# A recurrent layer and a mixture of experts on one core: more PSUM banks for the tiles, six weight places, a new written order

## The chip, the core and the metric
The kernel runs on one core of a Trainium2 chip. The core has five engines that run their own instruction streams and wait for each other by semaphores: TensorE (PE; its weight loads are shown apart as PEld), VectorE (DVE), ScalarE (ACT), GpSimd (POOL) and SyncE (SP). Here SP only issues DMAs, POOL issues the indirect DMAs (scatters), and DMA engines move the data. TensorE writes into PSUM, of which this kernel uses eight banks of 128 partitions x 512 floats; the other engines copy results from there into SBUF. The metric is the time of one execution on the device, in microseconds (us).

## The reference
All is in float32, x is 4 x 512 tokens of 256 features. First x + attention(layernorm(x)), then x + ffn(layernorm(x)):

```python
# attention: a gated linear recurrence with complex state
xh = x @ W_in + b_in
gate_x = sigmoid(block_diag_linear(xh, W_gx, b_gx))      # 8 blocks
gate_a = sigmoid(block_diag_linear(xh, W_ga, b_ga))
a = exp(complex(-8 * gate_a * softplus(a_real), a_imag * gate_a))
xc = sqrt(1 - a * a) * complex(xr, xi) * gate_x          # xr, xi: the halves of xh
h = linear_scan(a, xc)                                    # over the 512 tokens
out = concat(h.real, h.imag) @ W_out + b_out
# ffn: 32 experts in 8 groups; each token takes its best 6 out of its best 4 groups
scores = sigmoid(xf @ gate_w.T)
w, idx = top 6 of the scores in the best 4 groups; w = w / sum(w) * 2.5
y = sum over the token's experts e of w[e] * (silu(x @ w11[e].T) * (x @ w33[e].T)) @ w22[e].T
shared = (silu(xf @ sw1.T) * (xf @ sw3.T)) @ sw2.T
return y + shared
```

An expert's inner size is 128, the shared expert's is 2 x 128.

## The kernel before
**Stage 1, per batch b of 512 tokens.** `tokens_of`, `gates`, `angles`, `turned` and `scans` (named g, a, f and s with the number of the batch) compute the recurrence: statistics of the tokens (L335), the input product (L393), the gates, the angles' sine and cosine on ACT and DVE (L405 to L475), the scans on DVE. `attend` and `scored` (t) add the residual with transposes by the identity (L603) and the output product, normalize (L349), transpose (pt, L357) and compute the router's scores (pl, L516). `route` (r) picks the experts on DVE, computes a position `pos` for each of a token's six copies and lets POOL scatter the token's row of 320 floats (256 features, its weights, its place) into the table `xg` in DRAM, where each expert has an area of its own (L578). That is 24 scatters of 128 rows for a batch, 96 in all. In batches 0 and 1 a small memset on POOL (L588, 0.41 us) follows each scatter, to keep them at a distance. `shared` (h) computes the shared expert (sg and su at L637, sy at L646) and stores it to DRAM through SP (512 KB, L648).

**Tables.** `tables` (L650 to L717) turns the counts of tokens by expert into tables of tiles: which expert a tile of 128 rows belongs to, and where its rows lie. It is made twice: "ne" after batch 2 for the first 40 tiles (EARLY), "nl" for the others after batch 3. Each time it is a chain of some 20 small DVE operations with three PE operations between them: the count pc, a transpose ptt (L703) and a broadcast pb (L710).

**Stage 2, the tiles.** 112 tiles in 56 pairs p. Names: l, x, k, u, d.
- `read` (l, L820): SP loads a pair's rows from `xg`, two DMAs of 160 KB; four pairs ahead (AHEAD). Pairs 0 to 19 wait for the 72 scatters of batches 0 to 2, later ones for all 96.
- `spread` (x): four transposes on PE into one bank `pxt` (L836), a copy by ACT (L838) into one of two SBUF buffers, and four DVE operations, oh, pick, cd and place (L841 to L848).
- `weights` (k, L856): two DVE copies of an expert's w11 and w33 out of `w_all`, chosen by a register, into the next of the places `b_w`. Place number is tile number modulo the count of places, which is four here.
- `up` (u): eight matmuls into `gu` (L868), of two PE instructions each in the profile (16 rows), silu on ACT (L870), a multiply on DVE (L872).
- `down` (d): two matmuls into one bank `y` (L881; four rows in the profile), two ACT copies with the routing weight as scale (L885) into one of six places `b_y` (u, p, th, kk, s, c in turn), and two scatters by POOL into `zz` (L887).

Beside some pairs, `own_read` (o) loads the residual and the shared expert's result of a batch (2 x 512 KB) and `own_sum` (q, L923, 1.22 us on DVE) adds them.

**Last stage.** Once all scatters into `zz` have landed, `zz` is loaded in 16 DMAs into `w_all` (17 us on the chain), DVE sums the six results of a token (L978, L980), PE transposes them together with the own sum (pz, L984, L985), ACT copies (L987), SP stores.

**PSUM.** The eight banks belong to pools: ps_a has two ("a": stage 1's transposes and products, the tables' ptt and pb, the last stage's pz), ps_x two ("x1": the residual of stage 1, the last shared expert's sy), ps_s two ("gu"), ps_m one ("m": pxt) and ps_y one ("y").

**The order.** Nothing is left to a scheduler's taste: `ORDERS` is a written list for each engine, such as "x0:4 x1:4 u0:8", which reads: four instructions of x0, four of x1, eight of u0. `in_order` ties each instruction to the one before it on its engine. So an instruction that waits holds up all that stand behind it in its engine's list.

Of the kernel before, what the change touches and what calls it, by code (L numbers as in the profile page):

```python
# [9 lines left out]
F32 = mybir.dt.float32  # L10
# [9 lines left out]
P = 128  # L20
B, T, D = 4, 512, 256
KC = D // P
# [34 lines left out]

ORDERS = {
    ET.PE:
        "g0:8 t0:7 g0 t0 g0:15 g1:23 g2 g1 g2:5 t0:5 g2:2 t0:15 t1:2 t0 t1 t0 t1 t0:2 t1:4 t0:8 h0:3 g2:2 h0 g2 r0:2 g2 "  # L60
        "r0:4 g2:12 h0:2 g3:8 h0 t1:2 h0 t1:14 h0:8 t1:8 h1:2 t1 t2:2 t1 h1 t1:6 r1:2 t2:5 h1 g3:2 t2 g3:6 r1:4 g3:5 h1 "
        "g3:3 t2:3 h1 t2:13 h1:9 t2 h1 t2:8 h2:4 t2:7 r2 h2:4 r2:5 t3:3 h2:2 t3 ne h2 t3:2 h2:5 t3:9 ne t3:3 d0 t3:2 ne "
        "t3:13 h3 t3 h3:3 t3:6 h3 r3 h3:3 r3:5 h3:8 x0:4 x1:4 u0:8 u1:2 x2:4 u1:6 x3 u2 d0 x3 d0 x3 u2 x3 u2:5 d1 u2 d1 "
        "nl x4:2 u3:4 x4:2 u3:2 d2 u3:2 x5:4 u4 d2 u4:4 x6:3 u4:3 x6 d3:2 u5:3 x7:3 u5:3 x7 u5:2 u6:2 d4:3 u6:4 x8:4 "
        "u6:2 u7 d5:2 u7:3 x9:2 u7:2 x9:2 d6 u7:2 d6 u8:8 d7:2 u9:2 x10:4 u9:5 d8 u9 d8 x11:4 nl d8 u10:5 x12:4 u10 "
        "d9:2 u10:2 u11:8 x13:2 d10:2 u12 x13:2 u12:6 x14 u12 x14:3 u13:2 d11 nl u13:3 d11 x15:3 d12 x15 u13:3 u14:2 "
        "d12:2 u14 x16:4 u14:5 u15 d13 u15:2 d13 u15:5 x17:4 d14:2 u16:4 x18:2 u16 x18:2 u16:3 u17 d15 u17 d15 u17:6 "
        "d16 u18:6 x19:4 u18 d16:2 u18 u19:3 x20 u19 x20:3 u19 d17:2 u19:2 x21:2 u19 u20:2 x21:2 d18:2 u20:2 x22:4 "
        "u20:4 u21:2 d19:2 u21:6 u22 d20 u22:2 d20:2 x23 u22 x23:2 u22 x23 u22:3 d21:2 x24:2 u23 x24:2 u23:6 x25:2 u23 "
        "u24 x25:2 d22:2 u24:4 x26:4 u24 d23 u24 d23 u24 u25:8 d24:3 u26:6 x27:4 d25:2 u26:2 u27:3 x28:4 u27:2 d26:2 "  # L70
        "u27:2 x29:2 u27 x29:2 u28:6 x30:2 u28:2 x30 d27:2 x30 u29:6 d28 u29:2 u30 x31:2 d28 x31:2 d28 u30:7 d29:2 "
        "x32:4 u31:5 d30:2 u31:3 x33:4 u32:8 d31:2 d32 u33 x34:4 u33:7 u34:2 x35:4 d32:2 u34:6 x36:4 d33:2 u35:3 x37 "
        "u35:2 x37 u35:3 x37:2 d34:2 u36:8 d35:2 u37 x38:4 u37:7 u38 x39 d36:2 x39:2 u38 x39 u38 d36 u38:5 x40:4 u39 "
        "d37:2 u39:2 x41 u39:5 x41:3 u40:6 x42 d38:2 u40:2 x42:2 u41:4 x42 d39 u41:2 d39 x43 u41:2 d40 x43:2 u42:2 x43 "
        "u42:2 d40:2 u42 x44:2 u42 x44:2 u42:2 u43:4 d41 x45 d41 x45:2 u43:2 x45 u43:2 u44:3 d42:2 x46:2 u44 x46 u44:2 "
        "x46 u44:2 u45:2 d43:2 d44 u45 x47 u45:5 x47:3 d44 u46 d44 u46:7 x48:4 d45:2 u47:4 x49:2 u47:3 x49 d46 x49 d46 "
        "u47 u48:8 x50:3 u49:2 x50 d47:2 u49:2 x51 u49 x51 d48 x51 u49:2 x51 u49 d48:2 u50:7 d49:2 u50 u51 x52 u51 "
        "x52:3 u51:6 d50 x53:4 u52 d50 u52:7 d51 x54:4 d51 d52 u53:8 x55:2 d52:2 x55:2 u54:7 d53 u54 d53 u55:8 d54:2 "
        "d55:2",
    ET.DVE:  # L80
        "c cc:7 c:4 cc:2 c cc:5 g0 cc g0:6 c:2 cc:2 g0:2 c g0:13 c cc c g1 a0 g1 cc a0:2 g1 a0:2 cc g1:2 a0:3 g1:2 f0 "
        "g1 a0 g1 a0 g1 c g1:5 a0 g1:7 a0:2 f0 a0:3 f0 a0 f0:2 s0 a0:3 s0:8 g2 a1 g2:2 a1:2 g2:2 a1 t0 g2:2 t0 a1 t0 "
        "a1:3 f1 g2 t0:2 a1:2 t0:17 a1 f1 a1 f1 a1:4 f1 a1 f1 s1 r0:27 a1 r0:8 a1:2 s1:6 h0 f2 s1:2 g3 a2:2 g3:4 a2:5 "
        "t1 a2 t1 g3:2 h0 g3 a2 t1:13 r0 t1:7 a2 f2:2 a2:7 f2:2 s2 a2:2 r1:4 a2 r1:19 s2 r1:4 s2 r1:8 s2:4 r1 s2:2 a3:8 "
        "t2 h1 a3:2 t2 a3 t2:11 h1 t2:9 f3 a3 f3 a3:5 f3:3 s3 h2 a3:3 r2 s3:2 r2:5 s3 r2:30 h2 s3:2 ne s3:3 ne:16 k0 x0 "
        "t3:22 h3 k0 ne r3:25 h3 r3:9 x0 k0 k1 x0:2 k1 k2:2 u0 x1:4 r3:2 k3:2 x2:3 u1 k4 x2 x3:2 u2 k4:2 k5 x3:2 k5 "
        "x4:4 u3 k6 x5 u4 k6 x5:3 x6 k7:2 x6 k8 u5 k8 x6:2 x7 nl:2 u6 k8 k9 x7:3 x8:2 nl:2 k9 x8 nl x8 x9 nl u7 x9:3 "
        "x10 u8 x10 nl:2 k10 nl:10 k10 k11 x10:2 x11:4 u9 nl:2 k11 k12:3 u10 x12 nl k13:2 x12 q0 u11 x12:2 k14:2 x13:3 "
        "u12 u13 x13 x14 nl:2 k15:2 k16 x14 u14 nl x14 k16 x14 k16 x15:3 u15 k17:2 x15 x16:4 x17:2 u16 k18:2 k19 x17 "
        "k19 x17 u17 x18:2 k20 x18:2 k20 q1 x19:2 u18 x19 k20 u19 x19 x20 k21:2 k22:2 x20:2 u20 x20 x21:3 k23 x21 x22:2 "  # L90
        "u21 x22:2 x23:4 x24 k23 k24 q2 x24:2 k24:2 u22 x24 x25 u23 k25:2 k26:2 u24 k27 x25:3 x26:2 k27 u25 x26:2 k28 "
        "u26 x27:4 k28:2 k29:2 x28:3 u27 k30 u28 k30 k31:2 x28 x29:4 x30:2 u29 k32 u30 x30:2 x31:4 x32 k32:2 u31 k33:2 "
        "x32:3 x33 k34 x33:3 x34:2 u32 k34 k35:2 k36 u33 k36:2 x34:2 x35:3 u34 x35 x36 k37 x36:3 k37 u35 k38:2 x37:2 "
        "u36 x37:2 x38:4 x39 k39 u37 q3 x39:2 k39 k40:3 u38 x39 k41 x40:3 k41 x40 x41:2 u39 k42:2 u40 k43 x41 k43 x41 "
        "x42:2 k44 x42:2 x43 u41 x43:3 k44 x44:4 k44 k45 x45 u42 u43 u44 k45 k46:2 k47 x45:2 k47 x45 x46:3 u45 k48 x46 "
        "x47 k48:2 x47:2 u46 x47 x48:3 k49:2 u47 u48 k50 x48 x49:2 k50 u49 k51:2 x49:2 k52 x50:4 k52 x51:4 x52 u50 k52 "
        "u51 x52:2 k53:2 k54 u52 x52 x53 k54 x53:3 x54:4 x55:4 u53 k55:2 u54 u55",
    ET.Activation:
        "cc b0:2 g0:9 a0:2 g0:3 a0:8 g1:4 a0:2 g1:2 a0:2 g1:3 b1:2 g1 a1:2 b2:2 g1:2 a1:8 t0:4 p0:2 a1:2 t0:2 a1 t0 "
        "g2:4 a1 g2:4 h0 g2:2 a2:2 h0 b3:2 g2:2 a2:7 h0:2 t1:4 a2 t1 a2 t1 a2 p1:2 a2:2 t1 g3:7 h1 g3:2 a3:2 g3:3 a3 h1 "  # L100
        "a3:8 t2:4 h1 t2:2 a3 h1 a3 h2 a3 t2 p2:2 h2:3 t3:2 p3 t3:2 p3 t3:2 h3 t3 h3:2 x0 x1 u0 h3 x2 u1 d0:2 x3 u2 "
        "d1:2 x4 x5 u3 d2:2 x6 u4 d3:2 x7 u5 d4:2 u6 x8 d5:2 u7 x9 d6:2 u8 d7:2 x10 x11 u9 d8:2 d9:2 u10 x12 x13 u11 "
        "d10:2 x14 u12 d11:2 u13 x15 d12:2 x16 u14 d13:2 u15 x17 d14:2 u16 x18 d15:2 u17 x19 d16:2 u18 x20 d17:2 u19 "
        "x21 d18:2 x22 u20 d19:2 u21 d20:2 x23 u22 x24 d21:2 x25 u23 d22:2 u24 d23:2 x26 u25 d24:2 x27 d25 u26 d25 x28 "
        "u27 x29 d26:2 u28 x30 d27:2 u29 x31 d28:2 u30 d29:2 x32 u31 d30:2 x33 u32 x34 d31:2 x35 u33 d32:2 u34 x36 "
        "d33:2 u35 x37 d34:2 u36 d35:2 x38 u37 x39 d36:2 u38 x40 d37:2 x41 u39 d38:2 x42 u40 d39:2 x43 u41 d40:2 x44 "
        "u42 d41:2 u43 x45 d42:2 u44 x46 d43:2 u45 x47 d44:2 u46 x48 d45:2 x49 u47 d46:2 x50 u48 d47:2 u49 x51 d48:2 "
        "d49:2 u50 x52 u51 d50:2 x53 u52 x54 d51:2 u53 d52:2 x55 u54 d53:2 u55 d54:2 d55:2",
    ET.Pool:
        "c:10 r0:72 r1:71 r2:48 r3:24 d0:4 d1:4 d2:4 d3:4 r3:4 d4:4 d5:4 d6:4 d7:4 d8:2 r3:2 d8:2 r3:18 d9:4 d10:4 "  # L110
        "d11:4 d12:4 d13:4 d14:4 d15:4 d16:4 d17:4 d18:4 d19:4 d20:4 d21:4 d22:4 d23:4 d24:4 r1 d25:4 d26:4 d27:4 d28:4 "
        "d29:4 d30:4 d31:4 d32:4 d33:4 d34:4 d35:4 d36:4 d37:4 d38:4 d39:4 d40:4 d41:4 d42:4 d43:4 d44:4 d45:4 d46:4 "
        "d47:4 d48:4 d49:4 d50:4 d51:4 d52:4 d53:4 d54:4 d55:4",
    ET.SP:
        "c i0 c:3 i1 c:7 w:9 i2 w c:3 w c w:35 p0 w:19 i3 h0 p1 h1 p2 h2 l0 wl:7 p3 wl l0:2 l1:2 l2:2 l3:2 l4:3 l5:2 "
        "l6:2 l7:2 h3 l8:3 l9:2 l10:2 l11:2 o0 l12:3 o0 l13:2 o1 l14:2 l15:2 l16:3 l17:2 o1 l18:2 l19:2 l20:3 l21:2 "
        "l22:2 l23:2 o2:2 l24:3 l25:2 l26:2 l27:2 l28:3 l29:2 l30:2 l31:2 l32 o3 l32:2 l33:2 l34:2 l35:2 l36:3 l37:2 "
        "l38:2 l39:2 l40:3 o3 l41:2 l42:2 l43:2 l44:3 l45:2 l46:2 l47:2 l48:3 l49:2 l50:2 l51:2 l52:3 l53:2 l54:2 l55:2",
}


# [1 line left out]
def kernel(ctx, tc, x, w_in, w_gx, w_ga, vecs, w_out, gate, w11, w33, w22, sw1, sw3, sw2, out):  # L123
# [615 lines left out]
    for b in range(B):  # L739
        xh, gx, ga, u, p = made  # L740
# [34 lines left out]
    def again(tag, bufs, name, *shape):  # L775

        t = tmp.tile([P, *shape], F32, tag=tag, name=name, bufs=bufs)
        return t if len(shape) == 1 else t.rearrange("p a b -> p (a b)")
# [8 lines left out]
    b_gx, b_ga = again("gx", 2, "b_gx", T), again("ga", 2, "b_ga", T)  # L787
    b_sphi, b_cphi = again("sphi", 2, "b_sphi", T), again("cphi", 2, "b_cphi", T)
    b_y = [again(tag, 1, "b_" + tag, T) for tag in ("u", "p", "th", "kk", "s", "c")]
    b_w = [again(tag, bufs, "b_w" + tag, T) for tag, bufs in (("ph", 1), ("gx", 2), ("ga", 2), ("sphi", 2))]  # L790
    b_xt = [part_of(b_sphi, 0, 2, KC, P), part_of(b_cphi, 0, 2, KC, P)]
    b_silu = [part_of(b_gx, i, 2, P) for i in range(2)]
    b_act = [part_of(b_ga, i, 2, P) for i in range(2)]
# [33 lines left out]

    def spread(p):

        work(f"x{p}")  # L830
        rows = st[p][0]
        (_, et, had, _), t0 = of(2 * p)
        pt = ps_m.tile([P, 2, KC, P], F32, tag="m", name=f"pxt_{p}")
        for i in range(2):
            for k in range(KC):
                PE.transpose(pt[:, i, k], rows[:, i, k * P : (k + 1) * P], ident)  # L836
        xt = b_xt[p % 2]
        A.copy(xt, pt)  # L838
        oh = small.tile([P, 2, E], F32, tag="oh", name=f"oh_{p}", bufs=2)
# [35 lines left out]
    def down(p):  # L875
        work(f"d{p}")
        a, cd, place = st.pop(p)
        py = ps_y.tile([P, 2, D], F32, tag="y", name=f"y_{p}")
        for i in range(2):
            e = number(2 * p + i, 0, ET.PE, E - 1)  # L880
            m = PE.matmul(py[:, i], a[:, i], w2[:, bass.ds(e, 1)].rearrange("p o d -> p (o d)"), start=True, stop=True)  # L881
# [158 lines left out]
```

## Time and profile before

| what | value |
|---|---|
| median of 14 runs | 433.18 us (430.81 to 437.02) |
| the profiled execution | 433.95 us, span 432.0 us |
| busy in the span: PE, DVE, ACT, POOL | 350.1, 304.5, 234.6, 240.0 us |
| first scatter into `xg` issued | 80.71 us |
| last scatter of batch 2 issued, landed | 196.15, 198.64 us |
| first transpose of a tile, first matmul of a tile | 201.18, 204.95 us |
| last scatters into `zz` issued | 383.47 us |
| load of `zz` on the chain | 391.19 to 408.33 us |

The span goes from the first instruction to the last. The chain of work that ended last is followed back from the last instruction, at each step to what released it. In a table of waits, "A <- B" says that instructions A sat ready at the head of their engine until B ended. In a table of windows, the numbers behind each engine are the microseconds it was busy in that stretch and its instructions; the clock is TensorE's granted clock as a share of full speed. Of the 24 scatters of batch 3, twelve stand on POOL ahead of the first down result and the others among those of pairs 3 to 9.

### The profile page before, as it was taken

The numbers are of one execution on the slowest core, as the hardware profiler recorded it, in microseconds if no ns is written. First come the engines' busy times: TensorE is split into PE (matmuls) and PEld (weight loads), VectorE is DVE, ScalarE is ACT, GpSimd is POOL, SyncE is SP. The second block draws the span as 40 slices with busy tenths as digits, with TensorE's granted clock in tenths as the row PEclk, the third lists the DMA queues.
The fourth block names the chain that finished last, engine by engine and source line by source line (L and its number), as shares of the span: only waits on it lengthen the run. The fifth ranks groups of instructions, "written<-read, shape, count | busy, mean of one in ns | idle before, by whom it ended". The sixth has DMA issues, their size and how long they took to land.

```text
span 432.0 us, 7580 instructions
## 1 busy us (share of the span) xinstructions
PE 350.1 (81%) x2074; PEld 285.0 (66%) x2074; DVE 304.5 (70%) x991; ACT 234.6 (54%) x436; POOL 240.0 (56%) x269
## 2 busy tenths in 40 slices
PE   3925849997898878497999999999999999911394
PEld 3502336475636547355999999999999999911393
DVE  5179999999989997435668767766676576503883
ACT  2499699689769941341455455555555655510031
POOL 1000000498998998776777777777776667640000
PEclk9975988997999989779899999999999999975587
DMA  5799906524422344985877977946675564218995
GB/s 149 268 315 319 255 2 183 177 93 154 142 77 106 137 144 156 354 342 184 269 248 251 318 257 239 331 151 226 203 221 177 166 202 150 94 58 320 421 409 211
DMA packets 63580, 91.58 MB, mean 212 GB/s; under 512 B 8485, under 2 KB 53037, under 8 KB 63536
## 3 DMA queue, kind: packets, MB, share of 16 engines
q1 hardware_dynamic: 52400, 56.45, 41.3%
q0 software_dynamic: 9984, 28.33, 17.5%
q10 hardware_dynamic: 1152, 6.29, 3.6%
q8 instruction: 18, 0.29, 0.3%
q14 instruction: 26, 0.21, 0.2%
HBM read 51.19 MB, written 41.94 MB: 216 GB/s over the span
## 4 chain that ended last, share of the span: by engine, by line
PE 53%; DVE 20%; DMA 10%; ACT 8%; issue 5%; POOL 2%; ACTq 0%; SPq 0%; POOLq 0%; DVEq 0%
PE gu L868 22%; PE y L881 10%; PE pxt L836 5%; DMA w_all<-zz 4%; PE ph L393 3%; PE sg L637 2%; DMA zz<-b_u,place 2%; PE pz L984 2%; DMA xg<-row,pos 2%; PE pz L985 2%; POOL xg L578 1%; DVE st L335 1%; PE pt L357 1%; DMA x<-in_x_dram 1%; POOL zz L887 1%
## 5 line engine op out<-in xcount | busy, mean ns | idle before, releaser
L578 POOL DMA_INDIRECT xg<-row,pos x96 | 106.5, 1110 | 102.4 <-DVE w_all L474 78.3
L881 PE MATMUL y<-w_all,b_ga 128*128 x224 | 60.7, 381 | 0.9 <-ACT b_u L885 0.9
L872 DVE TENSOR_TENSOR b_ga<-b_gx,gu 128x256 f32<-128x256 f32 x56 | 23.4, 418 | 33.6 <-ACT b_gx L870 33.3
L881 PEld LDWEIGHTS y<-w_all,b_ga 128*128 128x128 f32 x224 | 36.9, 191 | 3.7 <-ACT b_u L885 1.3
L984 PE MATMUL pz<-ident,w_all 128*128 128x128 f32 x64 | 15.4, 330 | 27.9 <-DVE w_all L980 17.3
L870 ACT ACTIVATE b_gx<-gu 128x256 f32<-128x256 f32 x56 | 21.6, 385 | 29.0 <-PE gu L868 28.0
L868 PE MATMUL gu<-b_sphi,b_wgx 128*128 128x128 f32 x224 | 33.7, 281 | 0.0
L868 PE MATMUL gu<-b_cphi,b_wga 128*128 128x128 f32 x224 | 33.5, 278 | 0.0
L868 PE MATMUL gu<-b_sphi,b_wph 128*128 128x128 f32 x224 | 32.7, 277 | 0.0
L868 PE MATMUL gu<-b_cphi,b_wsphi 128*128 128x128 f32 x224 | 32.0, 275 | 0.0
L868 PEld LDWEIGHTS gu<-b_cphi,b_wga 128*128 128x128 f32 x224 | 30.9, 194 | 1.0
L984 PEld LDWEIGHTS pz<-ident,w_all 128*128 128x128 f32 x64 | 12.2, 237 | 28.9 <-DVE w_all L980 17.7
L868 PEld LDWEIGHTS gu<-b_sphi,b_wph 128*128 128x128 f32 x224 | 30.2, 192 | 1.1
L868 PEld LDWEIGHTS gu<-b_sphi,b_wgx 128*128 128x128 f32 x224 | 30.6, 197 | 0.5
L978 DVE TENSOR_TENSOR w_all<-w_all 128x768 f32<-128x768 f32 x16 | 15.1, 958 | 21.5 <-DMA w_all<-zz 21.4
L868 PEld LDWEIGHTS gu<-b_cphi,b_wsphi 128*128 128x128 f32 x224 | 29.1, 192 | 0.4
L987 ACT COPY o<-pz 128x256 f32<-128x256 f32 x16 | 5.9, 372 | 41.3 <-DMA w_all<-zz 26.9
L838 ACT COPY b_cphi<-pxt 128x512 f32<-128x512 f32 x28 | 16.4, 585 | 19.5 <-PE pxt L836 15.5
L838 ACT COPY b_sphi<-pxt 128x512 f32<-128x512 f32 x28 | 16.4, 586 | 15.4 <-PE pxt L836 13.0
L887 POOL DMA_INDIRECT zz<-b_u,place x20 | 20.0, 998 | 6.5 <-issue 2.1
L887 POOL DMA_INDIRECT zz<-b_p,place x20 | 20.0, 999 | 6.3 <-issue 1.7
L887 POOL DMA_INDIRECT zz<-b_th,place x18 | 18.3, 1018 | 8.6 <-ACT b_th L885 4.7
(331 smaller groups left out, 947.4 us busy)
## 6 DMA issues: line engine op xcount, KB each, us to landing
w_all<-in_w_dram SPq DMA_DIRECT2D x64, 128.0 KB
w_all<-zz SPq DMA_DIRECT2D x8, 768.0 KB
w_all<-zz ACTq DMA_DIRECT2D x8, 768.0 KB
xg<-blank SPq DMA_DIRECT2D x1, 5120.0 KB
b_xh<-xg SPq DMA_DIRECT2D x28, 160.0 KB
b_x<-xg SPq DMA_DIRECT2D x28, 160.0 KB
b_xn<-xg SPq DMA_DIRECT2D x28, 160.0 KB
b_xnt<-xg SPq DMA_DIRECT2D x28, 160.0 KB
```

The source lines that it names most:

```text
L393: PE.matmul(ph, win_sb[:, k, m * P : (m + 1) * P], xn[:, k], start=(k == 0), stop=(k == KC - 1))
L578: i = GP.indirect_dma_start(out=xg[:, :], out_offset=bass.IndirectOffsetOnAxis(ap=pos[:, t, k : k + 1], axis=0), in_=row[:, t], in_offset= ...
L637: PE.matmul(dst, w[:, i, k], xn2[:, k], start=(k == 0), stop=(k == KC - 1))
L836: PE.transpose(pt[:, i, k], rows[:, i, k * P : (k + 1) * P], ident)
L838: A.copy(xt, pt)
L868: PE.matmul(gu[:, w, i], w1[:, k, w], xt[:, i, k], start=(k == 0), stop=(k == KC - 1))
L870: A.activation(s, gu[:, 0], AF.Silu)
L872: V.tensor_tensor(a, s, gu[:, 1], ALU.mult)
L881: m = PE.matmul(py[:, i], a[:, i], w2[:, bass.ds(e, 1)].rearrange("p o d -> p (o d)"), start=True, stop=True)
L887: s = GP.indirect_dma_start(out=zz.rearrange("t k d -> (t k) d"), out_offset=bass.IndirectOffsetOnAxis(ap=place[:, i : i + 1], axis=0), in ...
L978: V.tensor_tensor(z[:, :half], z[:, :half], z[:, half:], ALU.add)
L984: PE.matmul(pt[:, k], z[:, 0, cut], ident, start=True, stop=False)
```

## The change
Three edits, and a new text of `ORDERS`.

```diff
-    b_w = [again(tag, bufs, "b_w" + tag, T) for tag, bufs in (("ph", 1), ("gx", 2), ("ga", 2), ("sphi", 2))]
+    b_w = [again(tag, bufs, "b_w" + tag, T) for tag, bufs in (("ph", 1), ("gx", 2), ("ga", 2), ("sphi", 2), ("cphi", 2))]
+    b_w.append(again("x", 2, "b_wx", KC, T)[:, :T])
...
     def spread(p):
...
-        pt = ps_m.tile([P, 2, KC, P], F32, tag="m", name=f"pxt_{p}")
+        more = p > 5 and p % 2
+        pt = (ps_a if more else ps_m).tile([P, 2, KC, P], F32, tag="a" if more else "m", name=f"pxt_{p}")
...
     def down(p):
...
-        py = ps_y.tile([P, 2, D], F32, tag="y", name=f"y_{p}")
+        more = p % 2
+        py = (ps_x if more else ps_y).tile([P, 2, D], F32, tag="x1" if more else "y", name=f"y_{p}")
```

So the transposes of odd pairs above 5 go to a bank of ps_a, the down results of odd pairs to a bank of ps_x, and the weight copies have six places, of which the two new ones lie in buffers of stage 1 that are free by then (42 of the 112 copies go there). The instructions are the same in number and kind; each engine's order is another. The parts around the start of the tiles, PE, DVE, POOL and SP in turn:

```diff
-h3:8 x0:4 x1:4 u0:8 u1:2 x2:4 u1:6 x3 u2 d0 x3 d0 x3 u2 x3 u2:5 d1 u2 d1 nl x4:2 u3:4 x4:2 u3:2 d2 u3:2 x5:4 u4 d2 u4:4
-x6:3 u4:3 x6 d3:2 u5:3 x7:3 u5:3 x7 u5:2 u6:2 d4:3 u6:4 x8:4 u6:2 u7 d5:2 u7:3 x9:2 u7:2 x9:2 d6 u7:2 d6 u8:8 d7:2
+h3:6 x0:4 h3:2 x1:4 u0:8 nl x2:4 u1:8 d0 x3:4 d0 u2:8 x4:4 d1 u3:6 d1 x5:4 u3:2 u4:2 d2:2 u4:6 d3 x6:2 d3 x6:2 d4 u5:8
+d4 nl u6:8 d4 nl x7:4 d5 x8:4 d5 d6:2 u7:5 x9 u7:3 x9:3 u8:2
...
-x4:4 u3 k6 x5 u4 k6 x5:3 x6 k7:2 x6 k8 u5 k8 x6:2 x7 nl:2 u6 k8 k9 x7:3 x8:2 nl:2 k9 x8 nl x8 x9 nl u7 x9:3
-x10 u8 x10 nl:2 k10 nl:10 k10 k11 x10:2 x11:4 u9 nl:2 k11 k12:3 u10 x12 nl k13:2 x12 q0 u11
+r3:6 x0 k0:2 k1:2 x0 r3:2 nl u0 k2 x0 x1:2 k2 k3 x1:2 k3 x2:2 u1 k4 x2:2 k4:2 x3:3 nl u2 x3 x4:2 nl:4 k5 nl k5 k6 x4 nl
+x4 u3 x5:2 k6 x5:2 x6 k7 nl x6 nl:6 u4 nl:3 k7 q0 k8 x6 nl:3 u5 x6 x7 k8:2 k9 u6 x7 nl:2 x7:2 x8:2 nl x8:2 k9 x9:2 k10:2 u7
...
-r2:48 r3:24 d0:4 d1:4 d2:4 d3:4 r3:4 d4:4 d5:4 d6:4 d7:4 d8:2 r3:2 d8:2 r3:18 d9:4 ... d24:4 r1 d25:4
+r2:48 r1 r3:22 d0:4 d1:4 d2:4 d3:4 d4:2 r3:6 d4:2 d5:4 d6:4 r3:16 d7:4 r3:4 d8:4 d9:4 ... d24:4 d25:4
...
-l4:3 l5:2 l6:2 l7:2 h3 l8:3 l9:2 l10:2 l11:2 o0 l12:3 o0 l13:2 o1 ... l32 o3 l32:2 ... l40:3 o3
+h3 l4:3 l5:2 l6:2 o0:2 l7:2 l8:3 o1 l9:2 l10:2 l11:2 l12:3 l13:2 o1 l14 o2 l14 l15 o2 l15 l16:3 ... l19 o3 l19 o3
```

(POOL and SP count two instructions to a scatter or a read.) In stage 1 the lists differ as well. On PE, two identity transposes of t0 instead of fourteen stand before the first pt of `gates`. On DVE, two memsets (L231, L238) stand before the first statistics. On ACT, batch 1's activation of L453 stands behind the normalization of batch 0's rows (L349) instead of ahead of it, and with it the later L459 and L465 of the same chain; the copies of batch 0's features (L358) still come behind L465. On SP one of the eight loads of w22 (wl) comes a little earlier.

## Prediction

> **What bounds the kernel now.** I began with the page's clock row and the summary of its chain of work that ended last:
>
> ```profile
> PEclk9975988997999989779899999999999999975587
> PE 53%; DVE 20%; DMA 10%; ACT 8%; issue 5%; POOL 2%; ACTq 0%; SPq 0%; POOLq 0%; DVEq 0%
> ```
>
> TensorE holds over half of the chain, with the clock full through most of the second half. An average over unlike stages says little, so I then asked for the windows (columns: length, PE, PEld, DVE, ACT, POOL busy, granted clock, DMA share, GB/s):
>
> ```profile
> 80.00:100.00 20.00, 19.79 (x76) 12.42 (x75) 19.40 (x44) 17.05 (x22) 17.59 (x22) 1.00 0.29 106
> 140.00:160.00 20.00, 15.38 (x58) 8.83 (x56) 19.08 (x56) 15.11 (x22) 18.14 (x23) 0.91 0.40 141
> 220.00:240.00 20.00, 20.00 (x156) 19.22 (x155) 15.27 (x68) 10.50 (x26) 15.26 (x16) 1.00 0.77 253
> 340.00:360.00 20.00, 20.00 (x158) 19.22 (x157) 11.22 (x38) 11.10 (x26) 12.93 (x14) 1.00 0.52 171
> ```
>
> From 220 to 360 us PE is busy 20.00 us in every 20 at a clock of 1.00: the tile stage is TensorE's own time. A pair of tiles is 16 gu rows (1.78 us), 4 y rows (0.87) and 4 transposes (0.44), 3.09 us; 56 pairs make 173 us, which is the distance from 204.95 us to the last matmul at about 378.8. A bank or a buffer more can take out of this only what PE waits for. So the third view is PE's waits from 180 to 405 us (total, times, longest):
>
> ```profile
> PE pz L984 <- DVE w_all L980: 17.3, 1, 17.3
> PE pt L357 <- ACT xs L624: 5.9, 1, 5.9
> PE pxt L836 <- DMA b_xh<-xg: 1.2, 2, 1.0
> PE pxt L836 <- DMA b_x<-xg: 1.1, 1, 1.1
> PE y L881 <- ACT b_u L885: 0.9, 1, 0.9
> PE pxt L836 <- ACT b_sphi L838: 0.8, 1, 0.8
> ```
>
> Two rows are waits for a PSUM bank, the last two, 1.7 us of 432. The others are for rows of tokens, the last stage's sum, and the router's input. Nothing here waits for a weight copy.
>
> What sets the start of the tiles is read from the chain in 172 to 240 us (start, length, what):
>
> ```profile
> 194.87 0.97 POOL xg L578
> 196.15 2.49 DMA xg<-row,pos
> 200.44 4.04 DMA b_x<-xg
> 204.51 0.44 PE pxt L836 x2
> 204.95 3.63 PE gu L868 x20
> ```
>
> The first tiles' reads wait for the 72 scatters of batches 0 to 2, which POOL issues one behind the other from 80.71 to 196.15. So three things can move the end: when POOL starts its scatters and how fast it goes, the ramp of the first tiles, and a new wait in a PE stream that has none.
>
> **Banks (pxt and py of odd pairs).** The 0.8 us is x1 waiting for the copy of x0 out of the one bank. After the change x1 still uses the old bank, as the new one is only for odd pairs above 5: gain 0. The 0.9 us is d55, which waits for ACT to empty d54's bank; d55 goes to a new bank, and the wait goes. But what is late next is POOL. The chain at the end shows:
>
> ```profile
> 378.25 0.97 POOL zz L887
> 380.91 8.47 DMA zz<-b_u,place
> ```
>
> POOL issues the last six scatters at 376.98, 378.25, 379.62, 380.91, 382.19 and 383.47, 1.28 us apart, and d55's two stand last whether their data is ready 0.9 us earlier or not. Gain 0 (at most 0.9, if POOL had caught up). In the middle there is no such wait to remove: 0. The last stage, from the scatters' landing to 432.0, keeps its instructions: 0.
>
> One rule of the Trainium skill speaks beside this: "TensorE: Matmul & The Clock Gate", section "HAM oscillation — how this bites in real kernels", reports that a second set of PSUM banks gave a stream already kept warm no further gain; by it too the banks are worth nothing, and this case's 20.00 of 20 says so with more right.
>
> **Six places for copied weights.** The 112 copies (L856, 128x512, 0.42 us) stay; 42 of them write the new places. PE's list has no wait for them, so 0. What hides a copy is PE's 3.09 us for a pair against DVE's work for it: two copies, the multiply (0.42) and the four small ones of spread (0.22, 0.29, 0.29, 0.16), 2.2 us.
>
> **Order of PE, tile start.** Two matmuls of the last shared expert (sy, 0.38 us each) move from before the first transposes to behind the first four. The short windows there, same columns:
>
> ```profile
> 203.00:204.50 1.50, 0.39 (x2) 0.15 (x2) 0.78 (x4) 0.00 (x0) 1.20 (x2) 1.00 0.89 242
> 206.00:207.00 1.00, 1.00 (x7) 1.00 (x6) 0.68 (x1) 0.00 (x0) 0.69 (x2) 0.50 1.00 371
> 209.00:210.00 1.00, 1.00 (x12) 1.00 (x11) 0.90 (x5) 0.59 (x1) 0.69 (x2) 1.00 0.43 159
> ```
>
> The clock is 0.50 from about 205.5 to 209.0, just behind a stretch, 201.0 to 204.5, in which PE was busy 1.29 of 3.5 us. Half rate for 3.5 us costs 1.75 us. The two matmuls raise 1.29 to 2.05. If that keeps the clock up, 1.75 us are won; if not, nothing; I take −0.4, nearer to nothing, since 2.05 of 3.5 is still a gap. The same page, section "Part 1: The HAM clock gate", would have the clock fall only after an idle window of about 3.4 us. No PE gap here was above 1.13 us, and it fell: the trace differs. By the page's rule the clock could not have fallen before and nothing could be won.
>
> **Order of DVE, PE and ACT in stage 1.** Batch 0's path to its positions: two memsets (L238 0.33, L231 0.17) stand before the first statistics, +0.50; twelve of the fourteen identity transposes that PE did ahead of the first pt go behind it (0.11 each at full clock, partly in PE's idle), up to −0.5; ACT's L453 of batch 1 (0.61, on the chain at 63.73) goes behind the normalization of batch 0's rows (L349), and so L465, behind which the copies of batch 0's features (L358) stand, waits longer for its input, 0 to +0.6; the rest of that path keeps its operations. So batch 0's positions come at −0.5 to +1.2; I take +0.8, nearer to the two costs that lie on the chain for certain. POOL goes without a break after that, so all of it reaches the tiles' start. Batch 1's positions are ready 0.1 us before POOL asks and have one 0.67 us operation less ahead of them, batch 2's have 4 us in hand: 0.
>
> How fast POOL goes is the unknown. Its groups, first from 80 to 167 us (batches 0 and 1), then from 167 to 200 (batch 2):
>
> ```profile
> L578 POOL DMA_INDIRECT xg<-row,pos x49 | 60.0, 1225 | 86.5 <-DVE w_all L474 78.3 <-issue 7.6 <-ACT so L647 0.5
> ...
> L578 POOL DMA_INDIRECT xg<-row,pos x25 | 24.6, 985 | 9.1 <-issue 8.2 <-ACT so L647 0.3 <-DMA xg<-row,pos 0.3
> ```
>
> The same instruction takes 1225 ns where DVE is busy 19 of 20 us and 985 where it is not: 48 × 0.24 = 11.5 us are lost beside DVE. The new order puts other DVE operations beside other scatters. Which, no row tells; the sum of DVE's work is the same, so I take 0, and a third of the loss, 3.8 us, to either side.
>
> "SBUF — State Buffer", section "Who interferes with whom", of the skill gives the cause: GpSimd and some DVE operations lock each other out of a shared port. It names 620 ns against some 3100. By that ratio a scatter beside DVE would be five times as long; the 1225 beside 985 says a quarter, so the row decides.
>
> **Order of DVE, tile start.** The tables for later tiles (22 or so operations, starts 0.14 apart in before at 233.38 to 235.65) and the first sum of shared results (L923, 1.22 us) move from beside pairs 7 to 15 to beside pairs 0 to 7, ahead of multiplies that PE's d4, d5 and d6 wait for. Between u3's last matmul and u4's PE needs u4 1.78 + d2 0.43 = 2.2 us. DVE in that time has x5's four (1.02), two copies (0.84), two of x6 (0.57), seven of the table (about 1.1) and u4's multiply (0.42), 3.9; it falls back 1.7. From u4's last matmul to d4's first, PE has d3 0.43 + x6 0.44 + u5 1.78 = 2.65, of which silu (0.38), multiply and passing on take 1.0: 1.6 in hand. So d4 comes about on time. Behind u4's multiply come six more of the table, the 1.22, two copies, one of x6 and u5's multiply, some 3.6 to PE's 2.65: it falls back a further 1.0, with a wait at d4's second half, where the table's own matmul stands between (behind it are x7, d5, d6). By durations the waits come to 1.5 us, by starts (8 to 15% closer) to 0. I take +0.8, the middle; below nothing it can't go, since DVE gets only more to do here. In the middle of the stage the DVE gets this time back, where nothing waits.
>
> **Order of POOL and SP.** POOL's distance memset (0.41) leaves the tile stage for the front of batch 3's scatters, which nobody waits for before pair 20. Down results 0 to 8 come among other counts of batch 3's scatters: at d7, eight more are ahead (8 × 1.28 = 10 us), so its place is free at about 250 us where d13 writes it at about 252.5: 2.5 us in hand. SP's store of the last shared result (512 KB) goes ahead of the rows of pair 4: rows at 211.5 to 212.4 where they are needed at 212.9. Both 0, but with little in hand.
>
> **Sum** against the profiled execution (433.95 us, span 432.0): +0.8 − 0.4 + 0.8 = +1.2, 435.15. That run lies 0.77 above the median 433.18 of the runs shown, so as a median: 434.4 us.
>
> **Rivals.**
> A, the forecast (0.46): the small sums above, 434.4, between 432 and 436.
> B, faster (0.20): the new order puts fewer long DVE operations beside POOL's scatters (−3.8) or keeps the clock at the tile start (−1.75, not −0.4). 434.4 − 3.8 is 430.6; with part of the clock, 430. For it speaks the 11.5 us that lie there; against it, that DVE has no less to do.
> C, slower (0.24): the tables and own sum at the head of DVE's tile work. Each microsecond by which u4's or u5's multiply comes after d4's or d5's turn is one of PE, which has no other slack. It decides from 1.6 us behind u4's last matmul's earliest multiply; with the copies and the read of the own sum (2 × 512 KB beside DMA at 0.8 of its time) 2 to 3 us later than summed, 437.
> D, slower (0.10): POOL is late, by scatters stretched by 3.8 us or d7's place missed by d13: 437.5.
> That the change doesn't do what it says is no rival: the instructions of the new kernel, set against the old, differ as told.
>
> A measurement of this kernel can tell 0.5% from no change, 431.0 to 435.35. A lies mostly within (0.42 of its 0.46, the rest above); B is faster; C and D are slower. Faster 0.20, same 0.42, slower 0.38. The range, leaving out a tenth at each end: 430.0 to 438.0.
>
> **What would show it.** The first L578 at 81 to 82 us, its mean near 1225; the first gu within 2 us of 205; PE's waits without y <- b_u and without new rows above 1 us; windows from 240 on still 20.00 of 20. A first gu before 203 or after 208 makes B or D right; PE rows y L881 or pb waiting for DVE between 215 and 235 make C right. Wrong altogether would be a PE that idles in mid-stage.

## The result and the profile after

The changed kernel takes 440.17 us (median of 10 runs, 437.57 to 443.2) against 432.96 (47 runs) for the kernel before: 1.0174 times, interval 1.0148 to 1.0199. It is slower by 7.2 us; 434.4 was forecast, and 440.17 lies above the range's 438. The profiled execution took 439.68 us with a span of 437.8. Its line numbers are 2 higher than before in stage 1 and 4 or 5 higher in the tiles.

The page's clock row and the summary of the chain, as shown of before:

```profile
PEclk9995896989989899969999998999999999985688
PE 43%; DMA 7%; issue 3%; DVE 1%; ACT 1%; POOL 1%; ACTq 0%; POOLq 0%; DVEq 0%
```

They hardly tell where the time went. The windows of the changed kernel do (length, PE, PEld, DVE, ACT, POOL busy, clock, DMA share, GB/s):

```profile
80.00:100.00 20.00, 15.57 (x53) 8.12 (x52) 16.33 (x37) 12.37 (x16) 14.46 (x19) 0.91 0.74 234
140.00:160.00 20.00, 15.83 (x55) 9.38 (x53) 18.52 (x47) 17.68 (x27) 17.97 (x24) 0.91 0.34 117
220.00:240.00 20.00, 20.00 (x157) 18.90 (x156) 16.87 (x72) 10.20 (x24) 15.93 (x14) 1.00 0.96 320
260.00:280.00 20.00, 17.58 (x125) 16.56 (x124) 10.92 (x39) 9.49 (x22) 15.36 (x15) 0.91 0.70 235
```

The last of these windows in the kernel before:

```profile
260.00:280.00 20.00, 20.00 (x159) 19.27 (x158) 15.22 (x51) 10.80 (x26) 15.14 (x16) 1.00 0.87 283
```

Two stretches differ most from before. From 80 to 100 us PE has 53 instructions where it had 76, and the DMA engines are busy 0.74 of the time where it was 0.29. From 260 to 280 us PE is busy 17.58 us, not 20.00, at a clock of 0.91.

The chain at the start of the tiles (start, length, what):

```profile
208.58 0.44 PE pxt L840 x4
...
210.36 1.79 PE gu L872 x16
```

The first gu stands at 210.36 against 204.95, 5.4 us later, and eight gu matmuls take 1.79 us at once: the clock is full from the first one. PE's waits from 180 to 405 us:

```profile
PE pz L989 <- DVE w_all L985: 17.0, 1, 17.0
PE pt L359 <- ACT xs L626: 6.4, 1, 6.4
PE gu L872 <- ACT b_cphi L842: 2.4, 1, 2.4
```

The two waits for a PSUM bank are gone, as are those for rows. One new wait has come, and it falls into the second stretch.

**The first stretch, 80 to 100 us.** I followed PE there. Its timeline after (start, length, engine, line, what, and in brackets how long it stood idle and who released it):

```profile
94.39 1.30 PE L372 MATMUL px<-ident,x 128*128 128x128 f32 x5 [4.43 <-DMA x<-in_x_dram]
```

PE waits 4.43 us for the input x of batch 3. Before, it came to these transposes at 87.00 us and found x there:

```profile
87.00 1.24 PE L370 MATMUL px<-ident,x 128*128 128x128 f32 x8
```

Who loads it? SP, whose timeline before was

```profile
51.62 0.47 SPq L263 DMA_DIRECT2D w_all<-in_w_dram  x1
67.14 0.37 SPq L625 DMA_DIRECT2D zx<-xs  x1
...
77.86 0.47 SPq L264 DMA_DIRECT2D w_all<-in_w_dram  x1
78.43 0.41 SPq L164 DMA_DIRECT2D x<-in_x_dram  x1
```

and after

```profile
43.98 0.47 SPq L266 DMA_DIRECT2D w_all<-in_w_dram  x1
69.30 0.37 SPq L627 DMA_DIRECT2D zx<-xs  x1
...
88.88 0.47 SPq L266 DMA_DIRECT2D w_all<-in_w_dram  x1
89.45 0.41 SPq L166 DMA_DIRECT2D x<-in_x_dram  x1
```

The store of batch 0's residual (zx<-xs, p0 in the list) waits for a copy that ACT makes at about 67 us (68 to 69 after). Before, SP issued weight loads until 52 us and only then stopped at the store, and 19 loads were left between it and x: "p0 w:19 i3". The new list says "p0 w:36 i3": SP stops at 44.5 us, stands idle for 25 us, and then has 36 loads of some 0.5 us each to issue before x. The load of x comes 11 us later, and a stream of weight loads runs just ahead of it. What hangs on PE's wait is read one engine at a time:

```profile
95.51 0.43 DVE L337 BATCH_NORM_STATS2 st<-px 128x6 f32<-128x256 f32 x1 [2.96 <-PE px L372]
```

```profile
100.34 0.72 ACT L445 ACTIVATE kk<-ph,magic 128x512 f32<-128x512 f32 x1 [3.94 <-DVE ph L444]
```

```profile
129.36 0.98 POOL L580 DMA_INDIRECT xg<-row,pos  x1 [4.43 <-issue]
```

DVE waits for PE with batch 3's statistics, and ACT's angles of batch 2 wait for DVE, as in a list each waits for all ahead of it. So batch 1's rows come 7.4 us later than before (their last normalization starts at 111.0 against 103.6 us), and with them its positions, and POOL, which had needed no pause between batch 0 and batch 1, stands still.

**The second stretch, 260 to 280 us.** ACT and PE:

```profile
263.45 0.84 ACT L890 ACTIVATE b_p<-y,cd 128x256 f32<-128x256 f32 x2 [4.05 <-DMA zz<-b_p,place]
```

```profile
264.81 1.22 PE L872 MATMUL gu<-b_cphi,b_wcphi 128*128 128x128 f32 x4 [2.42 <-ACT b_cphi L842]
```

ACT waits 4.05 us to write d13's result into place p, which POOL's scatters of d7 still hold; the copy of the next tiles' transposes stands behind it, and PE behind the copy. The clock pays for it as well:

```profile
264.00:266.00 2.00, 1.19 (x5) 1.19 (x6) 1.21 (x5) 1.52 (x4) 1.55 (x2) 0.68 0.39 143
266.00:268.00 2.00, 2.00 (x12) 2.00 (x11) 0.38 (x2) 0.47 (x1) 1.39 (x3) 0.50 0.67 205
```

Half rate for some 3.4 us behind a pause of 2.4 us makes the pause cost about 4.1 us in all. In "TensorE: Matmul & The Clock Gate", section "Part 1: The HAM clock gate", the Trainium skill lets the clock fall after an idle window of about 3.4 us. This pause was shorter, so the measurement decides, here as at the tiles' start before.

POOL's groups answer to those shown of before, batches 0 and 1 first, then batch 2:

```profile
L580 POOL DMA_INDIRECT xg<-row,pos x48 | 55.4, 1155 | 92.5 <-DMA w_all<-in_w_dram 80.3 <-issue 12.1 <-ACT sphi L425 0.2
```

```profile
L580 POOL DMA_INDIRECT xg<-row,pos x24 | 24.1, 1003 | 9.2 <-issue 9.2
```

A scatter beside DVE takes 1155 ns, 70 less than before: 3.4 us saved over 48, lost again in the pause. The end is the old one, with the landing and the load of zz a little shorter:

```profile
388.60 6.94 DMA zz<-b_u,place
397.34 16.42 DMA w_all<-zz
```

### The profile page after: what moved, and what is told of

It is laid out like the page before. It is cut to its first block, busy times and chain, and to the rows that moved or that the text cites. A ratio compares the mean times of both kernels' runs of the same rounds, so it can differ in the third digit from the quotient of the medians.

```text
span 437.8 us, 7553 instructions
## 1 busy us (share of the span) xinstructions
PE 350.4 (80%) x2074; PEld 284.5 (65%) x2074; DVE 302.3 (69%) x991; ACT 233.2 (53%) x436; POOL 239.8 (55%) x269
## 4 chain that ended last, share of the span: by engine, by line
PE 43%; DMA 7%; issue 3%; DVE 1%; ACT 1%; POOL 1%; ACTq 0%; POOLq 0%; DVEq 0%
PE gu L872 20%; PE y L886 9%; PE pxt L840 5%; DMA w_all<-zz 4%; PE pz L989 2%; PE pz L990 2%; DMA zz<-b_u,place 2%; DMA zz<-b_p,place 1%; DMA b_xh<-xg 1%; PE sg L639 1%; PE su L639 1%; PE sy L648 1%; PE pt L359 1%; POOL xg L580 1%; PE pl L518 0%
## 5 line engine op out<-in xcount | busy, mean ns | idle before, releaser
L580 POOL DMA_INDIRECT xg<-row,pos x96 | 104.4, 1088 | 113.1 <-DMA w_all<-in_w_dram 80.3
L892 POOL DMA_INDIRECT zz<-b_p,place x20 | 21.0, 1049 | 6.1 <-issue 3.1
L850 DVE TENSOR_REDUCE cd<-pick 128x4 f32<-128x128 f32 x56 | 15.8, 282 | 9.7 <-ACT b_p L890 3.4
L892 POOL DMA_INDIRECT zz<-b_c,place x18 | 18.8, 1042 | 5.6 <-issue 2.4
L395 PE MATMUL ph<-xn,win_sb 128*128 128x512 f32 x32 | 20.9, 813 | 1.1 <-ACT xn L360 1.1
L892 POOL DMA_INDIRECT zz<-b_kk,place x18 | 17.9, 994 | 6.6 <-issue 2.7
L892 POOL DMA_INDIRECT zz<-b_s,place x18 | 18.4, 1025 | 5.5 <-issue 2.4
L605 PE MATMUL x<-ident,x 128*128 128x128 f32 x64 | 13.2, 326 | 8.9 <-ACT xs L626 8.3
L590 POOL MEMSET idle<- 1x384 bf16 x48 | 19.6, 407 | 0.0
L605 PEld LDWEIGHTS x<-ident,x 128*128 128x128 f32 x64 | 10.9, 226 | 12.4 <-ACT xs L626 9.5
```

Source lines behind the costliest of these rows:

```text
L395: PE.matmul(ph, win_sb[:, k, m * P : (m + 1) * P], xn[:, k], start=(k == 0), stop=(k == KC - 1))
L580: i = GP.indirect_dma_start(out=xg[:, :], out_offset=bass.IndirectOffsetOnAxis(ap=pos[:, t, k : k + 1], axis=0), in_=row[:, t], in_offset= ...
L590: paced = GP.memset(idle, 0.0)
L605: PE.matmul(outs[j][:, k * P : (k + 1) * P], xb[:, k, cut], ident, start=(j % 2 == 0 and k == 0), stop=False)
L892: s = GP.indirect_dma_start(out=zz.rearrange("t k d -> (t k) d"), out_offset=bass.IndirectOffsetOnAxis(ap=place[:, i : i + 1], axis=0), in ...
```

## The experiments

Times are medians; ratios are to the kernel before, run on the same chip at the same time, with their intervals. A ratio is not the quotient of the two medians and can differ from it by up to 0.4%. The chip of the second four runs (e7 to e10) took 498.47 us for the kernel before, where the others took 433 to 434; those runs are compared only with each other.

| run | us | ratio | interval |
|---|---|---|---|
| e1 old orders, new banks and places | 432.81 | 0.9993 | 0.9965 to 1.0020 |
| e2 old stage 1 | 432.50 | 0.9966 | 0.9932 to 1.0000 |
| e4 old POOL | 439.41 | 1.0138 | 1.0097 to 1.0180 |
| e5 old stage 1 and POOL | 431.86 | 0.9969 | 0.9946 to 0.9993 |
| r1 the changed kernel again | 440.47 | 1.0158 | 1.0075 to 1.0242 |
| r2 batch 3's x early | 435.55 | 1.0036 | 0.9993 to 1.0080 |
| r3 x early, angles first | 435.34 | 1.0028 | 0.9989 to 1.0067 |
| r4 e1 with slower scatters | 437.41 | 1.0108 | 1.0030 to 1.0187 |
| c1 the kernel before, batch 3's x late | 441.38 | 1.0164 | 1.0113 to 1.0215 |
| c2 old SP and DVE in stage 1 | 442.98 | 1.0224 | 1.0165 to 1.0282 |
| c3 old SP, PE, ACT in stage 1 | 438.72 | 1.0101 | 1.0031 to 1.0170 |

**e1, the banks and places alone.** All five lists of before, in the changed kernel, with one condition altered, since in the old list x7's transposes stand ahead of the late tables, which use the same banks:

```diff
-        more = p > 5 and p % 2
+        more = p > 20 and p % 2
```

> The order of before on all five engines, with the new banks and the six weight places. (The transposes alternate from pair 21 on, as the old order makes the late tables behind x7's place.) Theory (two orders cost the time, the banks nothing): 433 us, within 1 us of before, with the wait of d55 for its bank (0.9 us) gone and POOL's last scatter where it was. Rival (a bank or a weight copy that is shared with another use adds waits): 436 us or more, with new rows among PE's waits.

0.9993: the banks and places are worth nothing that can be measured, as forecast. The rival falls. (Here the transposes use the new bank from pair 21 on; e5 below has it from pair 7 on and loses nothing either.)

**e2, e4 and e5, halves of the order.** The new lists, with stage 1's instructions in the old sequence (PE, DVE, ACT and SP), with POOL's list old, and with both.

> The changed kernel with the old order of stage 1's instructions on PE, DVE, ACT and SP; the tiles' order and all of POOL's stay new. Theory (stage 1 costs about 5 us, POOL's place for d7 about 4, independently): first gu near 204, d13's ACT copy still waits for the scatters of d7, total about 435. Rival (d13 waits only because the stage before is late): that wait gone, about 431. Rival (the tile order of DVE costs the time, not stage 1): 438 or more.

> The changed kernel with the old order on POOL alone. Theory: the wait of d13's ACT copy and the fall of the clock behind it go, about 4 us: 436, with first gu still near 210. Rival (the scatters of batch 3 only stop another pair): a wait of the same size at d9 or d15, 439 to 440.

> Both at once: old stage 1 and old POOL, new order of the tiles on PE, DVE, ACT and SP, new banks and places. Theory (the two add up): 431 to 433, at or a little below before, as PE's clock at the first tiles may stay up (1.75 us). Rival (a third cost in the tiles' order or the banks): 435 or more.

e2 gives back all 7 us, more than I had expected of stage 1 alone; e4 gives back next to none. The wait at d13 is still there in e2 (PE 2.1 us for the copy behind it, 2.4 in the changed kernel), so its rival, that the wait goes with the late stage 1, falls too. POOL's list decides where PE waits, not how much time is lost: with the old list another wait turns up. In e4 PE's waits from 180 to 405 us are

```profile
PE pt L359 <- ACT xs L626: 6.5, 1, 6.5
PE pxt L840 <- DMA b_x<-xg: 2.0, 2, 1.2
PE pxt L840 <- DMA b_xh<-xg: 0.6, 2, 0.3
```

where the last two are the rows of pairs 20 and 21 (at 270 to 273 us), which are read only when all of batch 3's scatters have landed. My theory of two independent costs fell here, in favour of: stage 1 decides, and POOL's work is a floor whatever its list, that is, the tiles can go no faster than POOL scatters. e5 (0.9969) and e2 (0.9966) cannot be told apart, and both are within 0.4% of the kernel before.

**e7, e8 and e9, single moves in the changed kernel** (e10 is below). In SP's list x (i3) goes up, in DVE's six instructions of batch 1's angles go ahead of batch 0's statistics:

```diff
-p0 w:36 i3
+p0 w:19 i3 w:17
...
-s0:8 a1:2 f1 t0 g2 a1:3 g2:2 a1:3 t0:2
+s0:8 a1:2 f1 a1:6 t0 g2:3 t0:2
```

> The changed kernel with one instruction moved: SP issues the load of batch 3's x after 19 of the 36 weight loads that stand behind the store of batch 0's residual, as in before, and not after all 36. Theory (that load came at 89.45 us against 78.43, and PE stood 4.4 us at the transposes of batch 3's x with batch 1's path behind them): PE's wait goes, the first scatter stays at 84.0, the tiles start 4 to 5 us earlier, 435.5 us. Rival (the DVE, ACT and PE orders of stage 1 hold the same place anyway): 439 or more.

> The changed kernel with six instructions moved on DVE: the end of batch 1's angle sums (L439 to L444) goes ahead of batch 0's statistics, which wait for PE. Theory (ACT's 5.2 us wait for L444 makes batch 0's positions 2 to 3 us late): that wait shrinks by 2 to 3 us, the first scatter comes at 81.5 to 82, but PE's wait for batch 3's x at 94 us stays, as the load's time hangs on the store of batch 0's residual: 438 to 440. Rival (the delay of the first scatters reaches the end in full): 437. Rival (the statistics, now behind the six, delay the rows by as much): 440 or more.

> Both moves at once. Theory (the two waits are the whole cost of the new stage 1): 433 to 434, a gu first at 203 to 204. Rival (more of the stage's order costs): 435 or more.

On the chip of 498 us they took 504.74, 508.84 and 504.44 us (1.0107, 1.0214, 1.0100 times before). The changed kernel was not run there, so only the order among them says something: the DVE move adds nothing to the move of x. So e7, e9 and e10 were run again beside the changed kernel:

> The changed kernel itself, beside the single moves, since the chip of the last four runs took 498 us for the kernel before, and comparisons between the two chips tell nothing. Expected by both theories: 1.017 times before.

> The move of batch 3's x load once more, on the chip of the changed kernel's own run. Theory (the late load costs 4 to 5 us): 0.99 times the changed kernel, about 1.006 times before, with no PE wait for that load. Rival: equal to the changed kernel.

> Both moves once more. Theory (the two waits are the whole cost of the new stage 1): 1.00 to 1.003 times before. Rival (more of the order costs): 1.005 or more.

One load moved gives 440.47 to 435.55, 4.9 of the 6.5 us above the 433.96 of the kernel before beside them. SP's timeline of r2 has it at

```profile
79.68 0.38 SPq L166 DMA_DIRECT2D x<-in_x_dram  x1
```

and PE has no wait at all from 80 to 100 us. r3 is no faster than r2 by more than the interval: ACT's wait for the angles of batch 1 shrinks from 5.4 to 3.1 us, but the first scatter comes only 0.7 us earlier (82.76 against 83.42). New waits of ACT for DVE take 1.5 of the 2.3 us (1.1 for L446, 0.4 for the rows' statistics, now behind the six), so the rival of e8 holds in part.

**c1, the converse.** The kernel before, with one instruction moved and nothing else of the change, the store p0 by 17 weight loads:

```diff
-w:35 p0 w:19 i3
+w:18 p0 w:36 i3
```

> The kernel before with one instruction moved: SP's store of batch 0's residual stands 17 weight loads earlier, so that 36 of them, and not 19, stand between it and the load of batch 3's x, as in the changed kernel. No bank, place or other order is changed. Theory (that place alone is most of the loss): the load issues 8 to 9 us later, PE waits for it at about 87 us, and the kernel takes 1.009 to 1.013 times before. Rival (the load is late only together with the rest of the new order): 1.000 to 1.004.

1.0164, more than I had expected and as much as the whole change (1.0174), from one position in one list. The 17 weight loads come later here too, as in the change; r2 leaves them late and moves x alone, so what it wins, 4.9 us, is the load of x. In c1 the store issues at 67.01 us, SP then has the 36 loads, and PE shows

```profile
93.83 0.44 PE L371 MATMUL px<-ident,x 128*128 128x128 f32 x1 [6.15 <-DMA x<-in_x_dram]
```

The wait is longer than in the changed kernel (6.15 against 4.43), because here PE came to it earlier. The scores of batch 1 come 8.6 us later than before, the first scatter of batch 3 8.1 us, the last scatter into `zz` 7.8.

**e10 and r4, is POOL a floor?** e1's kernel, with a memset behind each of the last twelve scatters of batch 3:

```diff
-                if b < B - 2:
+                if b < B - 2 or (b == B - 1 and t >= NT // 2):
                     paced = GP.memset(idle, 0.0)
```

> Order of before with the new banks and places (transposes alternate from pair 21 on), and a POOL memset of 0.41 us behind each of the last twelve scatters of batch 3, a period of 1.54 instead of 1.28 us: POOL gets 3.2 us more to do ahead of pair 20, PE, DVE and ACT nothing. Theory (POOL's chain of scatters is a floor under pairs 13 to 20, and gives back there what the tiles' start gains): 3 us more than with the banks alone, 436. Rival (POOL has time in hand there): 433.

> The memsets behind batch 3's last twelve scatters once more, on a chip as fast as that of the run with the banks alone (0.9993 times before). Theory (POOL's scatters are a floor under pairs 13 to 20): 3 us more than that run, 1.006 to 1.007 times before, with PE or ACT waiting at pairs 13 to 21. Rival (time in hand): 1.00.

e10 on the chip of 498 us made 495.68 (0.9982), no loss; that is inconclusive, as PE isn't full in the tiles there (40.33 of 50 us from 250 to 300). On a chip of the usual speed r4 stands at 1.0108 against e1's 0.9993, and its profiled execution has a span of 434.5 us against e1's 431.5. The theory holds in kind; by the span the price is 3.0 us for 3.2 of POOL's time, by the ratios 5 us with a wide interval, so its size is not settled. The clock had no part in it: from 250 to 285 us it stayed at 1.00 in r4. ACT's waits in r4 for places that scatters still hold:

```profile
260.30 0.47 ACT L889 ACTIVATE b_kk<-y,cd 128x256 f32<-128x256 f32 x1 [2.93 <-DMA zz<-b_kk,place]
273.74 0.47 ACT L889 ACTIVATE b_u<-y,cd 128x256 f32<-128x256 f32 x1 [3.89 <-DMA zz<-b_u,place]
```

The profiled executions side by side show the floor. The columns are shifts against before, in us: POOL's first scatter of batch 3, and silu of pairs 15 and 21.

| run | first scatter of batch 3 | u15 | u21 |
|---|---|---|---|
| changed | +9.4 | +4.4 | +8.5 |
| e1 | +0.3 | -2.9 | +1.4 |
| e2 | -0.6 | -1.4 | +2.4 |
| e4 | +9.7 | +5.8 | +9.6 |
| e5 | -1.3 | -0.3 | +0.6 |
| r2 | +3.8 | -1.1 | +4.3 |
| r4 | -1.8 | -1.6 | +4.4 |

Wherever PE stands at pair 15, at pair 21 it is where POOL's scatters let it be, within some 3 us of their own shift (r4 has 3 to 5 us of memsets more). Behind it the shifts change by little (the changed kernel's last pairs stand at +7 to +8).

**c2 and c3, the rest of stage 1.**

> The changed kernel with the old stage 1 order on SP and DVE; PE and ACT keep the new one. Single moves left 1.003, the whole old stage 1 gave 0.997. If DVE's order holds the difference: 0.997 to 0.999. If PE's or ACT's holds it: 1.002 to 1.004.

> The changed kernel with the old stage 1 order on SP, PE and ACT; DVE keeps the new one. If PE's and ACT's order hold the difference: 0.997 to 0.999, the first scatter at 80 to 81 us. If DVE's holds it: 1.002 to 1.004, the first scatter near 83.

Neither theory holds: both mixtures have batch 3's x early, like r2, and stand above it, c2 clearly, c3 with an interval that overlaps r2's; and both are slower than e2, which has the old list on all four engines. In c2 the scores of batches 1 and 2 are 3.5 to 3.9 us late and batch 3's 9.7; in c3 PE waits 10.1 us for rows (L351) where it was 7.8, and batch 3's scores are 7.6 late. I read this as lists that are made for each other, so that half of the old with half of the new loses what the whole old one has; no run shows which pair of lists clashes. Which engine's order holds the 0.6 to 0.7% between e2 and r2 or r3 stays open.

## Why the prediction was wrong

**The step that failed is the one on the order of stage 1.** It weighed DVE, PE and ACT there, and for SP only the store ahead of pair 4's rows. The text put batch 1's positions at "0", as they had 0.1 us in hand and less DVE work ahead. They came 7.3 us late, by a load that stands behind a waiting store in SP's list. The description of the change has the same gap: for SP in stage 1 it names a load of w22 and not the store p0. The two lists were there to read, "p0 w:19 i3" and "p0 w:36 i3", and the trace of before had all prices: the store cannot go before ACT's copy at about 67 us, 17 loads at 0.5 us each are 8.6 us more between it and x, and PE's first use of x stood at 87.00 us, 8.6 behind the issue of the load. A term of some +8 for the load, less what PE had in hand, would have been the largest of the sum. c1 shows it alone: the load issues 9.5 us later, PE waits 6.15 us for it, and the kernel takes 7.4 us more.

The other steps:
- Banks and places at 0: right (e1). PE's waits for banks went, and the end stayed POOL's.
- The middle at 0, "no wait to remove": right for what was there, but the step took full PE for a sign that nothing stands close behind. POOL does: e1's tiles ran 2.9 us ahead up to pair 15 and lost 4.3 by pair 21.
- Order of POOL and SP, d7 with 2.5 us in hand: wrong by the late batch 3, whose scatters began 9.4 us later while the tiles began only 5.4 later. d7's second scatter went at 260.15 us (236.50 before; some 10 us more were forecast), and d13 waited. As rival D it was named, with the right place, but its price is not POOL's list: e4 took it away and won 0.8 us, less than the noise. D's sign, a first gu after 208, came true by luck: not by stretched scatters, which were shorter, but by batch 1's late positions.
- The clock at the tiles' start, -0.4: the full 1.75 came, but not by the two matmuls. PE was busy with the late batch 3 up to the first tile (2.00 of every 2 us from 204 on), so there was no gap. With stage 1 in its old order the clock fell in spite of the two matmuls' new place (e2: 0.50 from 202 to 204 us; e5: 0.50 from 202 to 206), and with the old tile order it stayed at 1.00 in e1 and fell in r4 (0.50 from 203 to 206). The tiles gained at first (silu of pair 5 at +2.8 us, the first gu at +5.4) and lost it by pair 21 (+8.5).
- DVE at the tiles' start (+0.8, and rival C): it did not happen. PE's waits have no row for DVE in the tiles, and none of d4, pb or d6 was late.
- Batch 0's start, +0.8: measured +3.3 at the first scatter, of which r3 gives back 1.2 by both moves. ACT stood 5.2 us for DVE's angles of batch 1, which stand ahead of batch 0's rows in its list; before, it did not wait there:

```profile
60.90 0.72 ACT L445 ACTIVATE w_all<-w_all,magic 128x512 f32<-128x512 f32 x1 [5.18 <-DVE w_all L444]
```

And PE, idle for 1.35 us before the output product, ran eight of the matmuls at half rate (0.85 us a pair, not 0.43), which no step had.
- Scatters beside DVE, 0 within 3.8: they gained 3.4 us, and POOL spent it waiting for batch 1. That a shared port is what slows them, no run here shows.

## What to carry to other kernels

In an order written by hand, read every engine's list against the old one, the DMA queues first. An instruction that waits on an issuing queue holds all transfers behind it, and moving a store past loads moves the loads. Where one engine is full, ask which other is nearly so: a gain ahead of it only moves the wait to the place where the second one sets the pace.

## What the hardware showed that was not expected

A pause of PE of 2.4 us was followed by some 3.4 us at a clock of 0.50, which nearly doubled its price (260 to 280 us, changed kernel). In r4 pauses of 1.66 and 1.81 us, at 262 and 274 us, left it at 1.00. And one chip took 498.47 us for a kernel that others ran in 433 to 434, and the same slower scatters that cost 1.1% elsewhere cost nothing there: a ratio holds for the chip on which both were run.
